# A transformer block with conditioned norms: all softmax sums inverted on VectorE, and a feed-forward step's weights in two transfers

## The chip, the cores and the metric

The kernel runs on one core of one Trainium2 chip. A core has five engines that run their own instruction streams and wait for each other through semaphores: TensorE (PE in the profile; its weight loads are PEld), VectorE (DVE), ScalarE (ACT), GpSimd (POOL) and SyncE (SP), which here only issues transfers. SP, ACT and POOL issue transfers to the same 16 DMA engines. The metric is the device time of one execution in microseconds, of which the median over several runs is compared.

## The reference

`x` has 4 sequences of 1024 tokens with 512 features, all in float32. One transformer block is computed and added to its input:

```python
def _tc_rmsnorm(x, t, gw, gb, bw, bb):
    g = (t @ gw.T + gb)[:, None, :]
    b = (t @ bw.T + bb)[:, None, :]
    inv_rms = rsqrt(mean(x * x, axis=-1, keepdims=True) + 1e-6)
    return g * x * inv_rms + b

x1 = x + attention(_tc_rmsnorm(x, t, g1w, g1b, b1w, b1b))    # 16 heads of 32, softmax over all 1024 keys
x2 = x1 + swiglu(_tc_rmsnorm(x1, t, g2w, g2b, b2w, b2b))     # (silu(x @ gate.T) * (x @ hid.T)) @ out.T, 2048 hidden
return x + x2
```

The softmax is `exp(s - max) / sum(exp(s - max))`. The kernel doesn't divide each weight: it sums the exponentials over the keys, takes the inverse, and multiplies the attention output by it.

## The kernel before, in words

Tokens are cut into 8 blocks of 512 (`n`; `NBLK`), features into 4 chunks of 128, and the hidden features into 16 slices of 128 (`f`; `NF`). Activations lie with features on the 128 partitions and tokens along the row.

**Key steps.** The main loop runs over steps `g`. A step takes 256 keys of four heads against 256 queries. Four steps (`UN`; `kind = g % 4`) cover the 1024 keys: together they are one set `j` of sums (64 sets), and a group of four steps in the profile. Eight groups are a query block of 32 steps (`BS`). In step `g` PE makes the scores of step `g` (`scores`, L301); ACT copies them to SBUF (`keep`, L308); VectorE follows the running maximum (`running_max`, L313 and L316). Once the four steps of a set are there, PE transposes the maxima (`max_T`), VectorE reduces them and splits them in three bfloat16 parts (`parts`), PE transposes these (`parts_T`), ACT copies them (mT, L340), PE spreads them to all partitions (`spread`, L348) and ACT copies that (`shift`, L349). Five steps after the scores VectorE adds the negative maximum (`shifted`, L354) and ACT takes the exponential (`exponential`, L357); a step later PE multiplies with the values (`weighted`, L367), and a transfer issued by POOL accumulates the exponentials of a set into its first tile (`accumulate`, L381). VectorE folds the two halves (`fold_sum`, L389).

**The inverse of the sums.** At `kind == 0` three groups after the scores, `sums` (L399) adds over the keys with a matmul against ones, so that each head's 256 sums stand on 32 equal rows. `sums_out` (L406) copies them from PSUM (L408). For 55 of the 64 sets they then go by transfers: `compact` (L148) stores one row per head to DRAM from ACT's queue; two steps later `take` (L153), on ACT's queue, loads the 1024 sums as 128 rows of 8; `invert` (L160) takes the reciprocal of these on VectorE; `put` (L164), on ACT's queue in the next group's `kind == 0`, stores them; `sums_in` (L414), at that group's `kind == 1`, loads each head's inverses back onto 32 rows with four broadcast transfers on SP's queue (L173); `normalize` (L424) multiplies at that group's `kind == 3`. The last set of each query block but the last (`near`, L402), seven in all, skips the transfers: VectorE takes the reciprocal of all rows at `kind == 1` (L821), and `normalize` follows at `kind == 2`. The last two sets (`direct`) are inverted straight from PSUM (`inverse`, L419) at once.

**The feed-forward part.** From step `FS` = 60 on, two steps make a pass `p` (128 passes: 16 slices for each of 8 token blocks). A pass computes the gate and hidden features of one slice by a scheme with seven products in place of eight: it takes sums of weight quarters and sums of token quarters. The weight sums are made once, in steps 4 to 51: `weight_sums` (L470) loads the slice's gate and hid weights at the end of step `3f + 4`, and at the end of step `3f + 6` VectorE forms four sums and SP stores them to DRAM (`s_w`). `load_f` (L502) fetches a pass's weights in two parts of two transfers each, part 1 of pass `p + 1` in its even step and part 0 of pass `p + 2` in its odd step. The pass runs `pair_26`, `copy_156` (L545), `pair_7`, `sub_5` (L552) in the even step, and `pair_3`, `gate_tanh` (L562), `pair_15` of the next pass, `take_5` (L526), `gate` (L567), `add_15` (L530), `pair_4`, `hidden` (L570) in the odd one. The even step also holds `contract` with the output weights of an earlier pass, which `take_contract` (L583) adds to the residual.

**What sets the order.** The order on PE, VectorE, ACT and POOL is that of the program. Beside the steps, fixed actions are hung on step numbers (`pin` at the start of a step, `between` halfway, `after` at its end), and a queue of matmul chains (projections of queries, keys and values, 1.5 a step) fills the steps before `FS`. Keys are asked for three steps ahead of use, values three, queries two, the residual (`load_res`, 1 MB) at the seventh step of a query block. SP issues loads and stores in its own order, each once its tile is free.

**Buffers.** Tiles of one tag share a ring. Tag `fw` (five of 4 KB a partition) holds `wkq`, the weights and sums in `weight_sums`, and the weights of the passes. Tag `h` (seven of 2 KB) holds what the projections stage for their stores before `FS`, and the hidden features after it. Tag `w` is two PSUM banks for sums, projections, `pa` and `pc`.

Of the kernel before, what the change touches and what calls it, by code (L numbers as in the profile page):

```python
# [10 lines left out]
F32 = mybir.dt.float32  # L11
BF16 = mybir.dt.bfloat16
AF = mybir.ActivationFunctionType
ALU = mybir.AluOpType
# [3 lines left out]
P = 128  # L18
# [6 lines left out]
def tile_cond_transformer_block(  # L25
# [122 lines left out]
    def compact(tag: str, t, rows: int, n: int):  # L148

        inv_s[tag] = tc.dram_tile([P // rows, n], F32, name=f"sums{tag}")  # L150
        nc.scalar.dma_start(out=inv_s[tag], in_=t[0:P:rows, :])
# [17 lines left out]
    def spread_inverse(tag: str, t, rows: int, n: int):  # L169

        src = inv_s.pop(tag).rearrange("(h p) c -> h (p c)", p=rows)
        for h in range(P // rows):
            nc.sync.dma_start(  # L173
                out=t[h * rows : (h + 1) * rows, :], in_=src[h : h + 1, :].to_broadcast([rows, n])
            )
# [47 lines left out]
    def load_wkq(hg: int):  # L223
        t = sb.tile([P, 2, C, P], F32, tag="fw", name=f"wkq{hg}", bufs=5)
        nc.sync.dma_start(out=t, in_=kq_w[hg])
        wkq[hg] = t
# [164 lines left out]
    def take_av(j: int):  # L391
        avs[j] = sb.tile([P, HQ], F32, tag="avs", name=f"avs{j}", bufs=3)
        nc.scalar.copy(avs[j], av.pop(j))
# [7 lines left out]

    def near(j: int):  # L402

        return j % (C * NB // HQ) == C * NB // HQ - 1 or j >= NR // UN - 2

    def sums_out(j: int):  # L406
        t = sb.tile([P, HQ], F32, tag="rec", name=f"total{j}", bufs=2)
        nc.scalar.copy(t, state.pop(("sum", j)))  # L408
        if near(j):
            state["rec", j] = t  # L410
        else:
            compact(f"s{j}", t, DH, HQ)

    def sums_in(j: int):  # L414
        t = sb.tile([P, HQ], F32, tag="rec", name=f"rec{j}", bufs=2)
        spread_inverse(f"s{j}", t, DH, HQ)
        state["rec", j] = t

    def inverse(j: int):  # L419
        rec = sb.tile([P, HQ], F32, tag="rec", name=f"rec{j}", bufs=2)  # L420
        nc.vector.reciprocal(rec, state.pop(("sum", j)))  # L421
        state["rec", j] = rec

    def normalize(j: int):  # L424

        m, qh = divmod(j, NB // HQ)
        n, hg = divmod(m, C)
        rec = state.pop(("rec", j))
        if (n, hg) not in oT:
            oT[n, hg] = sb.tile([P, NB], F32, tag=f"oT{hg}", name=f"oT{m}")  # L430
        nc.vector.tensor_tensor(oT[n, hg][:, qh * HQ : (qh + 1) * HQ], avs.pop(j), rec, ALU.mult)

# [37 lines left out]
    def weight_sums(f: int, step: int):  # L470
        if step == 0:
            state["gh", f] = sb.tile([P, 2, C, P], F32, tag="fw", name=f"gh{f}", bufs=5)
            nc.sync.dma_start(out=state["gh", f], in_=gh_w[f])
        else:
            t = state.pop(("gh", f))
            a11, a12, a21, a22 = (t[:, i, k : k + 2, :] for i in range(2) for k in (0, 2))
            o = sb.tile([P, 4, 2, P], F32, tag="fw", name=f"s{f}", bufs=5)
            nc.vector.tensor_tensor(o[:, 0], a21, a22, ALU.add)
            nc.vector.tensor_tensor(o[:, 1], o[:, 0], a11, ALU.subtract)
            nc.vector.tensor_tensor(o[:, 2], a11, a21, ALU.subtract)  # L480
            nc.vector.tensor_tensor(o[:, 3], a12, o[:, 1], ALU.subtract)
            nc.sync.dma_start(out=s_w[f], in_=o)

# [17 lines left out]

    def load_f(p: int, part: int):  # L502
        f = p % NF
        fw[p, part] = sb.tile([P, 4, 2, P], F32, tag="fw", name=f"fw{p}_{part}", bufs=5)
        if part == 0:
            nc.sync.dma_start(out=fw[p, 0][:, 0:2], in_=gh_w[f][:, 0].rearrange("p (a c) o -> p a c o", a=2))
            nc.sync.dma_start(out=fw[p, 0][:, 2:4], in_=s_w[f][:, 0:2])
        else:
            nc.sync.dma_start(out=fw[p, 1][:, 0:2], in_=s_w[f][:, 2:4])
            nc.sync.dma_start(out=fw[p, 1][:, 2], in_=gh_w[f][:, 1, 2:4])  # L510

# [6 lines left out]
    def pair_15(p: int):  # L518
        b11 = tokens(p // NF)[0]
        a = bank_a[p] = ps.tile([P, NB], F32, tag="w", name=f"pa{p}")  # L520
        product(a[:, LEFT], fw[p, 0][:, 0], b11, True)
        product(a[:, RIGHT], fw[p, 0][:, 2], state["sums"][:, 0])

# [8 lines left out]
    def pair_26(p: int):  # L532
        a = bank_a[p]
        product(a[:, LEFT], fw[p, 0][:, 1], tokens(p // NF)[2])
        product(a[:, RIGHT], fw[p, 0][:, 3], state["sums"][:, 1])

# [10 lines left out]
    def pair_7(p: int):  # L547
        product(bank_b[p][:, RIGHT], fw[p, 1][:, 0], tokens(p // NF)[1])

# [4 lines left out]
    def pair_3(p: int):  # L554
        product(bank_a[p][:, RIGHT], fw[p, 1][:, 1], tokens(p // NF)[3])

    def pair_4(p: int):
        product(bank_b[p][:, LEFT], fw[p, 1][:, 2], state["sums"][:, 2])

# [143 lines left out]
    with tc.manual_schedule(  # L703
# [59 lines left out]

        def take_sums(j: int, j_before: int):

            if 0 <= j < NR // UN:
                sums(j)
                if j >= direct:
                    inverse(j)
                    normalize(j)  # L770
                else:
                    sums_out(j)
            if 0 <= j_before < direct and not near(j_before):
                put(f"s{j_before}")

        while g < END:
# [8 lines left out]
            n_on = 0 <= j_n < NR // UN  # L785
            j_o = g // UN - 4
            o_on = 0 <= j_o < direct
            ffn = g >= FS
# [8 lines left out]
            if kind == 1 and m_on:  # L797
                spread(j_m, 0)
            if kind == 3 and o_on and not near(j_o):
                normalize(j_o)  # L800
            if kind == 2 and n_on and near(j_n) and j_n < direct:
                normalize(j_n)
            if x_on and kind != 1:
# [14 lines left out]
            if g < NR:  # L818
                keep(g)
            if kind == 1 and n_on and near(j_n) and j_n < direct:  # L820
                nc.vector.reciprocal(state["rec", j_n], state["rec", j_n])  # L821
            if kind == 2 and n_on and not near(j_n):
                take(f"s{j_n}")
            if kind == 1 and s_on:
                take_av(j_s)
            due = bool(first) and first[0][0] <= g
            if not ffn:
# [3 lines left out]
                if kind == 0:  # L831
                    take_sums(j_n, j_o)
                if g < NR:
# [17 lines left out]
                if kind == 3 and s_on:  # L851
                    fold_sum(j_s)
                if g in (FS - 4, FS - 3):
                    load_f(0, g - FS + 4)
                if g == FS - 1:
                    load_f(1, 0)
            elif even:
                load_f(p + 1, 1)
                pair_26(p)
                copy_156(p)  # L860
                if kind == 0:
                    take_sums(j_n, j_o)
                if x_on:
# [16 lines left out]
            else:  # L880
                load_f(p + 2, 0)
                extra = due or len(queue) > FG
# [36 lines left out]
                for fn, a in halfway.pop(g, []):  # L919
                    fn(*a)  # L920
            if kind == 3 and n_on and not near(j_n):
                invert(f"s{j_n}")
            if kind == 1 and o_on and not near(j_o):
                sums_in(j_o)
            columns[0] = DH
# [13 lines left out]
        for p in range(p0, NP_):  # L939
            if p + 1 < NP_:  # L940
                load_f(p + 1, 1)
            pair_26(p)
            copy_156(p)
            if p == n * NF - 1:
                token_sums(n, 0)
                token_sums(n, 1)
                token_sums(n, 2)
            one, two, evict = filler(p, True)
            one()
            if p + 2 < NP_:  # L950
                load_f(p + 2, 0)
            pair_7(p)
            sub_5(p)
            pair_3(p)
            gate_tanh(p)
            gate(p)
            if p + 1 < NP_:
                pair_15(p + 1)
                take_5(p + 1)
                add_15(p + 1)  # L960
            pair_4(p)
            hidden(p)
            if p == n * NF - 1:
                token_sums(n, 3)
            two()
            evict()
            if p == p0:
                pm = ps.tile([P, NB], F32, tag="w", name=f"pmf{n}")
                for c in range(C):
                    nc.tensor.matmul(pm, ones_mean, squares[c], start=(c == 0), stop=(c == C - 1))  # L970
                inv = sb.tile([P, NB], F32, tag="tot", name=f"invf{n}", bufs=1)
                nc.scalar.activation(inv, pm, AF.Sqrt, bias=eps)
                nc.vector.reciprocal(inv, inv)
                state[f"f{n}"] = inv
            if p == p0 + 1:
                norm_rest(1, n // QB, x2[n], f"f{n}")
# [45 lines left out]
```

## Time and profile before

| | |
|---|---|
| median of 3 runs | 2523.32 us (2521.0 to 2535.55) |
| the profiled execution | 2529.8 us, its span 2528.0 us, mean granted clock of TensorE 0.986 |
| busy before 553 us (474 us from 79 on): PE, DVE, ACT | 447.1, 370.0, 330.2 us; DMA share 0.91 |
| busy from 553 to 2212 us (1659 us) | 1585.1, 1351.5, 996.9 us; DMA share 0.85 |
| busy from 2212 us to the end (316 us) | 303.3, 109.7, 49.9 us; DMA share 0.42 |
| transfers of sums | 165 from ACT's queue (4 KB each), 220 from SP's (32 KB each) |
| transfers of a pass's weights | 512: 256 of `fw<-sw`, 128 and 128 of `fw<-in_gh_w` |
| reciprocals | 55 of 128x8 (192 ns), 7 of 128x256 from SBUF (1744 ns), 2 from PSUM (1752 ns) |

A row such as `L354 DVE TENSOR_TENSOR raw<-raw,shift 128x2048 f32 ... x320 | 593.0, 1854 | 158.4 <-ACT shift L349 153.2` names the line, the engine, the operation, what it writes and reads by the program's tile names, how often, then busy us and mean ns of one, and the idle time of the engine just ahead of it with what ended most of it. In the timeline a bracket gives the idle time and its releaser. A q behind an engine's name (ACTq, SPq) marks what its sequencer does, such as issuing a transfer. PEclk is the share of TensorE's clock that was granted. The DMA share is the mean busy share of the 16 DMA engines.

### The profile page before, as it was taken

Reading aid. Unit: us, or ns where it says so; the run is one execution under the profiler, and the core shown is the slowest. Engines: PE = TensorE matmul, PEld = TensorE weight load, DVE = VectorE, ACT = ScalarE, POOL = GpSimd, SP = SyncE. Lnnn points to the kernel's source line nnn. Section 1 sums busy time; section 2 is a strip of 40 time slices with the busy share of each in tenths; the row PEclk is TensorE's granted clock in tenths of the full one; section 3 lists DMA queues with packets and bytes.
Section 4 is the critical chain, followed back from the end, with each engine's and each line's share of the span. In section 5 each row is a group of like instructions: output and inputs, shape, how many; then the busy total and the mean of one; then the engine's idle time right before and its main releaser. Section 6 shows DMA issues by size and latency. Waiting matters only on the chain. (4 is left out here: it accounts for less than half of the span.)

```text
span 2528.0 us, 72020 instructions
## 1 busy us (share of the span) xinstructions
PE 2404.4 (95%) x31749; PEld 1131.5 (45%) x31749; DVE 1854.4 (73%) x2180; ACT 1409.2 (56%) x1486; POOL 172.8 (7%) x207
## 2 busy tenths in 40 slices
PE   8989999999999899998999899989999899989999
PEld 3333333344444444544444444444444444434444
DVE  2677878777879786997788778978798768843332
ACT  3667776676556565665566556655565556512110
POOL 0000000000000000000000000000000000000000
PEclk9999999999999999999999999999999999999999
DMA  6599998999878887898879888888788888863442
GB/s 208 158 283 248 254 248 235 231 225 224 216 191 209 222 200 187 214 219 200 196 198 220 209 191 196 220 215 200 192 216 206 202 196 196 212 165 114 143 124 84
DMA packets 245085, 509.68 MB, mean 202 GB/s; under 512 B 44483, under 2 KB 125471, under 8 KB 217382
## 3 DMA queue, kind: packets, MB, share of 16 engines
q0 software_dynamic: 28656, 208.68, 42.8%
q1 hardware_dynamic: 197520, 295.66, 35.8%
q8 instruction: 251, 4.11, 0.6%
q10 hardware_dynamic: 18598, 0.74, 0.5%
q14 instruction: 60, 0.49, 0.1%
HBM read 253.87 MB, written 42.42 MB: 117 GB/s over the span
## 5 line engine op out<-in xcount | busy, mean ns | idle before, releaser
L354 DVE TENSOR_TENSOR raw<-raw,shift 128x2048 f32<-128x2048 f32 (+1 forms) x320 | 593.0, 1854 | 158.4 <-ACT shift L349 153.2
L357 ACT ACTIVATE raw<-raw 128x2048 f32<-128x2048 f32 x256 | 490.9, 1917 | 245.2 <-DVE raw L354 127.2
L308 ACT COPY raw<-sc 128x2048 f32<-128x2048 f32 x256 | 479.5, 1873 | 184.0 <-PE sc L301 147.4
L313 DVE TENSOR_TENSOR rmax<-rmax,raw 128x1024 f32<-128x1024 f32 x384 | 469.0, 1221 | 68.3 <-ACT raw L308 62.6
L106 PE MATMUL pc<-h,ow 128*32 128x512 f32 x4096 | 471.0, 597 | 7.5 <-DVE rec L421 5.0
L106 PE MATMUL pa<-x,fw 128*32 128x256 f32 x6144 | 388.4, 386 | 5.2 <-DVE pa L530 5.1
L367 PE MATMUL av<-raw,v 128*32 128x256 f32 x4096 | 278.4, 390 | 29.0 <-ACT raw L357 22.6
L381 POOL DMA_DIRECT2D raw<-raw x192 | 165.6, 863 | 2040.0 <-ACT raw L357 931.6
L301 PE MATMUL sc<-q,k 32*128 32x256 f32 x4096 | 293.3, 400 | 1.0 <-ACT raw L308 1.0
L106 PE MATMUL pa<-sums,fw 128*32 128x256 f32 x4096 | 268.0, 379 | 0.0
L106 PEld LDWEIGHTS pa<-x,fw 128*32 128x32 f32 x6144 | 193.1, 111 | 166.4 <-issue 30.5
L106 PEld LDWEIGHTS pc<-h,ow 128*32 128x32 f32 x4096 | 128.2, 110 | 254.1 <-issue 225.4
L106 PE MATMUL pkq<-y,wkq 128*32 128x512 f32 (+1 forms) x1664 | 231.6, 594 | 6.6 <-ACT y L187 4.1
L301 PEld LDWEIGHTS sc<-q,k 32*128 32x128 f32 x4096 | 184.9, 184 | 116.9 <-issue 68.7
L367 PEld LDWEIGHTS av<-raw,v 128*32 128x32 f32 x4096 | 107.9, 110 | 154.7 <-ACT raw L357 47.0
L106 PEld LDWEIGHTS pa<-sums,fw 128*32 128x32 f32 x4096 | 133.3, 110 | 88.9 <-issue 1.4
L545 ACT COPY pb<-pa 128x256 f32<-128x256 f32 x128 | 46.3, 362 | 203.2 <-PE pa L106 163.4
L583 DVE SCALAR_TENSOR_TENSOR res<-pc,res 128x512 f32<-128x512 f32 x128 | 88.1, 688 | 86.8 <-PE pc L106 86.7
L562 ACT ACTIVATE t<-pa 128x512 f32<-128x512 f32 x128 | 77.9, 608 | 109.5 <-PE pa L106 109.5
L106 PE MATMUL pb<-x,fw 128*32 128x256 f32 x2048 | 134.1, 379 | 4.2 <-ACT pb L545 4.1
L106 PE MATMUL pb<-sums,fw 128*32 128x256 f32 x2048 | 133.9, 379 | 0.0
L106 PEld LDWEIGHTS pkq<-y,wkq 128*32 128x32 f32 (+1 forms) x1664 | 73.3, 116 | 133.9 <-issue 121.8
(105 smaller groups left out, 1933.5 us busy)
## 6 DMA issues: line engine op xcount, KB each, us to landing
raw<-raw POOLq DMA_DIRECT2D x192, 1024.0 KB, 8.9
fw<-sw SPq DMA_DIRECT2D x256, 256.0 KB
fw<-in_gh_w SPq DMA_DIRECT2D x128, 256.0 KB
ow<-in_out_w SPq DMA_DIRECT2D x128, 256.0 KB
wkq<-in_kq_w SPq DMA_DIRECT2D x32, 512.0 KB
v<-vs SPq DMA_DIRECT2D x128, 128.0 KB
fw<-in_gh_w SPq DMA_DIRECT2D x128, 128.0 KB
k<-kqs SPq DMA_DIRECT2D x124, 128.0 KB
```

What stands on the lines that cost most here:

```text
L106: nc.tensor.matmul(dst[k : k + n, :], w[:, k : k + n], moving, start=start, stop=stop, skip_group_check=seeded)
L301: nc.tensor.matmul(sc[:, i, k, :], keys[rows, k * P : (k + 1) * P], queries[rows, :], start=True, stop=True)
L308: nc.scalar.copy(raw[r].rearrange("p k h q -> p h k q"), state.pop(("sc", r)))
L313: nc.vector.tensor_tensor(rmax[j], rmax[j], raw[r][:, k, :, :], ALU.max)
L354: nc.vector.tensor_tensor(t, t, s.unsqueeze(1).to_broadcast(list(t.shape)), ALU.add)
L357: nc.scalar.activation(raw[r], raw[r], AF.Exp)
L367: nc.tensor.matmul(av[j][i * DH : (i + 1) * DH, :], v[m, u][:, k, i * DH : (i + 1) * DH], raw[r][:, k, i, :], start=(kt == 0), stop=(kt == ...
L381: nc.gpsimd.dma_start(out=acc[j].rearrange("p k h q -> p (k h q)"), in_=raw[r].rearrange("p k h q -> p (k h q)"), accum_op=ALU.add,)
L545: nc.scalar.copy(bank_b[p][:, RIGHT], bank_a[p][:, RIGHT])
L562: nc.scalar.activation(state["t", p], bank_a[p], AF.Tanh, scale=0.5)
L583: nc.vector.scalar_tensor_tensor(r, pp, 0.5, r, ALU.mult, ALU.add)
```

## The change

Every set of sums is now copied from PSUM to SBUF by ACT and inverted in place by VectorE on all 128 rows (128x256); `near`, `sums_in` and the transfers for sums are gone. The reciprocal stands at the start of `kind == 2` ahead of `shifted`, `normalize` right behind it, but for the first set of a query block, whose `normalize` comes at `kind == 1` of the next group. The last two sets are inverted at once, as before, but from the copy. The weights of a pass come in two transfers: three quarters of the gate and hid weights (`fa`, 3 KB a partition), which the host has put in a row, and all four sums (`fw`, 4 KB). Both are asked for at the start of the even step of pass `p`, for pass `p + 2`. The tiles of `weight_sums` are halved and move from tag `fw` to tag `h`. Rings: `fw` from five to three (for `wkq` and the sums), `fa` new with three, `avs` from three to two. The transfers for the norms' roots are as before.

```diff
-        t = sb.tile([P, 2, C, P], F32, tag="fw", name=f"wkq{hg}", bufs=5)
+        t = sb.tile([P, 2, C, P], F32, tag="fw", name=f"wkq{hg}", bufs=3)
...
-        avs[j] = sb.tile([P, HQ], F32, tag="avs", name=f"avs{j}", bufs=3)
+        avs[j] = sb.tile([P, HQ], F32, tag="avs", name=f"avs{j}", bufs=2)
...
     def sums_out(j: int):
-        t = sb.tile([P, HQ], F32, tag="rec", name=f"total{j}", bufs=2)
-        nc.scalar.copy(t, state.pop(("sum", j)))
-        if near(j):
-            state["rec", j] = t
-        else:
-            compact(f"s{j}", t, DH, HQ)
-
-    def sums_in(j: int):
-        t = sb.tile([P, HQ], F32, tag="rec", name=f"rec{j}", bufs=2)
-        spread_inverse(f"s{j}", t, DH, HQ)
-        state["rec", j] = t
+        state["total", j] = sb.tile([P, HQ], F32, tag="total", name=f"total{j}", bufs=2)
+        nc.scalar.copy(state["total", j], state.pop(("sum", j)))
 
     def inverse(j: int):
-        rec = sb.tile([P, HQ], F32, tag="rec", name=f"rec{j}", bufs=2)
-        nc.vector.reciprocal(rec, state.pop(("sum", j)))
-        state["rec", j] = rec
+        nc.vector.reciprocal(state["total", j], state["total", j])
...
         if step == 0:
-            state["gh", f] = sb.tile([P, 2, C, P], F32, tag="fw", name=f"gh{f}", bufs=5)
-            nc.sync.dma_start(out=state["gh", f], in_=gh_w[f])
+            for i in range(2):
+                state["gh", f, i] = sb.tile([P, 2, 2, P], F32, tag="h", name=f"gh{f}_{i}", bufs=7)
+                nc.sync.dma_start(out=state["gh", f, i], in_=gh_w[f][:, 2 * i : 2 * i + 2])
...
+            o = [sb.tile([P, 2, 2, P], F32, tag="h", name=f"s{f}_{i}", bufs=7) for i in range(2)]
...
-            nc.sync.dma_start(out=s_w[f], in_=o)
+            for i in range(2):
+                nc.sync.dma_start(out=s_w[f][:, 2 * i : 2 * i + 2], in_=o[i])
...
-    def load_f(p: int, part: int):
+    def load_f(p: int):
         f = p % NF
-        fw[p, part] = sb.tile([P, 4, 2, P], F32, tag="fw", name=f"fw{p}_{part}", bufs=5)
-        if part == 0:
-            nc.sync.dma_start(out=fw[p, 0][:, 0:2], in_=gh_w[f][:, 0].rearrange("p (a c) o -> p a c o", a=2))
-            nc.sync.dma_start(out=fw[p, 0][:, 2:4], in_=s_w[f][:, 0:2])
-        else:
-            nc.sync.dma_start(out=fw[p, 1][:, 0:2], in_=s_w[f][:, 2:4])
-            nc.sync.dma_start(out=fw[p, 1][:, 2], in_=gh_w[f][:, 1, 2:4])
+        fw[p, 0] = sb.tile([P, 3, 2, P], F32, tag="fa", name=f"fa{p}", bufs=3)
+        nc.sync.dma_start(out=fw[p, 0], in_=gh_w[f][:, 0:3])
+        fw[p, 1] = sb.tile([P, 4, 2, P], F32, tag="fw", name=f"fw{p}", bufs=3)
+        nc.sync.dma_start(out=fw[p, 1], in_=s_w[f])
...
                 sums(j)
+                sums_out(j)
                 if j >= direct:
                     inverse(j)
                     normalize(j)
-                else:
-                    sums_out(j)
-            if 0 <= j_before < direct and not near(j_before):
-                put(f"s{j_before}")
...
-            if kind == 3 and o_on and not near(j_o):
-                normalize(j_o)
-            if kind == 2 and n_on and near(j_n) and j_n < direct:
-                normalize(j_n)
+
+            if kind == 2 and n_on and j_n < direct:
+                inverse(j_n)
+                if j_n % (BS // UN):
+                    normalize(j_n)
+            if kind == 1 and n_on and j_n % (BS // UN) == 1:
+                normalize(j_n - 1)
...
-            if kind == 1 and n_on and near(j_n) and j_n < direct:
-                nc.vector.reciprocal(state["rec", j_n], state["rec", j_n])
-            if kind == 2 and n_on and not near(j_n):
-                take(f"s{j_n}")
...
-                if g in (FS - 4, FS - 3):
-                    load_f(0, g - FS + 4)
-                if g == FS - 1:
-                    load_f(1, 0)
+                if g in (FS - 4, FS - 2):
+                    load_f((g - FS + 4) // 2)
             elif even:
-                load_f(p + 1, 1)
+                load_f(p + 2)
...
             else:
-                load_f(p + 2, 0)
...
-            if kind == 3 and n_on and not near(j_n):
-                invert(f"s{j_n}")
-            if kind == 1 and o_on and not near(j_o):
-                sums_in(j_o)
...
+    gh = np.stack([inputs_first(given["gate_w"]), inputs_first(given["hid_w"])], axis=2)
...
-        "gh_w": np.stack([inputs_first(given["gate_w"]), inputs_first(given["hid_w"])], axis=2),
+        "gh_w": gh.reshape(*gh.shape[:2], 4, 2, P)[:, :, [0, 1, 3, 2]],
```

More of the change, by code (lines that the diff above doesn't have):

```diff
@@ L400, in sums @@
         state["sum", j] = total
-    def near(j: int):
-        return j % (C * NB // HQ) == C * NB // HQ - 1 or j >= NR // UN - 2
     def sums_out(j: int):
-        t = sb.tile([P, HQ], F32, tag="rec", name=f"total{j}", bufs=2)
-        nc.scalar.copy(t, state.pop(("sum", j)))
-        if near(j):
-            state["rec", j] = t
-        else:
-            compact(f"s{j}", t, DH, HQ)
-    def sums_in(j: int):
-        t = sb.tile([P, HQ], F32, tag="rec", name=f"rec{j}", bufs=2)
-        spread_inverse(f"s{j}", t, DH, HQ)
-        state["rec", j] = t
+        state["total", j] = sb.tile([P, HQ], F32, tag="total", name=f"total{j}", bufs=2)
+        nc.scalar.copy(state["total", j], state.pop(("sum", j)))
     def inverse(j: int):
-        rec = sb.tile([P, HQ], F32, tag="rec", name=f"rec{j}", bufs=2)
-        nc.vector.reciprocal(rec, state.pop(("sum", j)))
-        state["rec", j] = rec
+        nc.vector.reciprocal(state["total", j], state["total", j])
     def normalize(j: int):
@@ L427, in normalize @@
         n, hg = divmod(m, C)
-        rec = state.pop(("rec", j))
+        total = state.pop(("total", j))
         if (n, hg) not in oT:
             oT[n, hg] = sb.tile([P, NB], F32, tag=f"oT{hg}", name=f"oT{m}")
-        nc.vector.tensor_tensor(oT[n, hg][:, qh * HQ : (qh + 1) * HQ], avs.pop(j), rec, ALU.mult)
+        nc.vector.tensor_tensor(oT[n, hg][:, qh * HQ : (qh + 1) * HQ], avs.pop(j), total, ALU.mult)
     def load_res(n: int):
@@ L471, in weight_sums @@
         if step == 0:
-            state["gh", f] = sb.tile([P, 2, C, P], F32, tag="fw", name=f"gh{f}", bufs=5)
-            nc.sync.dma_start(out=state["gh", f], in_=gh_w[f])
-        else:
[L475 to L481, printed above, removed]
-            nc.sync.dma_start(out=s_w[f], in_=o)
+            for i in range(2):
+                state["gh", f, i] = sb.tile([P, 2, 2, P], F32, tag="h", name=f"gh{f}_{i}", bufs=7)
+                nc.sync.dma_start(out=state["gh", f, i], in_=gh_w[f][:, 2 * i : 2 * i + 2])
+        else:
+            (a11, a12), (a22, a21) = (
+                (t[:, 0], t[:, 1]) for t in (state.pop(("gh", f, i)) for i in range(2))
+            )
+            o = [sb.tile([P, 2, 2, P], F32, tag="h", name=f"s{f}_{i}", bufs=7) for i in range(2)]
+            nc.vector.tensor_tensor(o[0][:, 0], a21, a22, ALU.add)
+            nc.vector.tensor_tensor(o[0][:, 1], o[0][:, 0], a11, ALU.subtract)
+            nc.vector.tensor_tensor(o[1][:, 0], a11, a21, ALU.subtract)
+            nc.vector.tensor_tensor(o[1][:, 1], a12, o[0][:, 1], ALU.subtract)
+            for i in range(2):
+                nc.sync.dma_start(out=s_w[f][:, 2 * i : 2 * i + 2], in_=o[i])
     def tokens(n: int):
@@ L521, in pair_15 @@
         product(a[:, LEFT], fw[p, 0][:, 0], b11, True)
-        product(a[:, RIGHT], fw[p, 0][:, 2], state["sums"][:, 0])
+        product(a[:, RIGHT], fw[p, 1][:, 0], state["sums"][:, 0])
     def take_5(p: int):
@@ L534, in pair_26 @@
         product(a[:, LEFT], fw[p, 0][:, 1], tokens(p // NF)[2])
-        product(a[:, RIGHT], fw[p, 0][:, 3], state["sums"][:, 1])
+        product(a[:, RIGHT], fw[p, 1][:, 1], state["sums"][:, 1])
     def copy_156(p: int):
@@ L547, in pair_7 @@
     def pair_7(p: int):
-        product(bank_b[p][:, RIGHT], fw[p, 1][:, 0], tokens(p // NF)[1])
+        product(bank_b[p][:, RIGHT], fw[p, 1][:, 2], tokens(p // NF)[1])
     def sub_5(p: int):
@@ L554, in pair_3 @@
     def pair_3(p: int):
-        product(bank_a[p][:, RIGHT], fw[p, 1][:, 1], tokens(p // NF)[3])
+        product(bank_a[p][:, RIGHT], fw[p, 1][:, 3], tokens(p // NF)[3])
     def pair_4(p: int):
-        product(bank_b[p][:, LEFT], fw[p, 1][:, 2], state["sums"][:, 2])
+        product(bank_b[p][:, LEFT], fw[p, 0][:, 2], state["sums"][:, 2])
     def gate_tanh(p: int):
@@ L762, in filler, with take_sums @@
             )
-        def take_sums(j: int, j_before: int):
+        def take_sums(j: int):
             if 0 <= j < NR // UN:
                 sums(j)
+                sums_out(j)
                 if j >= direct:
@@ L785, in tile_cond_transformer_block @@
             n_on = 0 <= j_n < NR // UN
-            j_o = g // UN - 4
-            o_on = 0 <= j_o < direct
             ffn = g >= FS
@@ L831, in tile_cond_transformer_block @@
                 if kind == 0:
-                    take_sums(j_n, j_o)
+                    take_sums(j_n)
                 if g < NR:
@@ L861, in tile_cond_transformer_block @@
                 if kind == 0:
-                    take_sums(j_n, j_o)
+                    take_sums(j_n)
                 if x_on:
@@ L939, in tile_cond_transformer_block @@
         for p in range(p0, NP_):
-            if p + 1 < NP_:
-                load_f(p + 1, 1)
+            if p + 2 < NP_:
+                load_f(p + 2)
             pair_26(p)
@@ L949, in tile_cond_transformer_block @@
             one()
-            if p + 2 < NP_:
-                load_f(p + 2, 0)
             pair_7(p)
```

## The prediction

> **What bounds the kernel now.** I read the page first (engines' busy shares), then the waits of TensorE (PE), then the timeline at its longest gaps, then the busy time in stretches of four key steps.
>
> ```profile
> PE 2404.4 (95%) x31749; PEld 1131.5 (45%) x31749; DVE 1854.4 (73%) x2180; ACT 1409.2 (56%) x1486; POOL 172.8 (7%) x207
> ```
>
> PE is busy for 95%, so at most 2528.0 - 2404.4 = 123.6 us of its gaps can be won, plus what it loses while its clock is low. PE's waits (who waited for whom: us in total, times, longest) say what the gaps are, and the longest wait of ScalarE (ACT) on a transfer, in the same view of all engines, what lies behind them.
>
> ```profile
> PE sp L348 <- ACT mT L340: 49.1, 8, 11.3
> PE av L367 <- ACT raw L357: 22.6, 23, 1.5
> ...
> PE pa L106 <- DVE pa L530: 5.1, 13, 0.7
> PE pc L106 <- DVE rec L421: 5.0, 2, 3.2
> ...
> PE pb L106 <- ACT pb L545: 4.1, 4, 1.6
> ```
>
> ```profile
> ACT raw L357 <- DMA sumss<-total: 79.7, 19, 15.4
> ```
>
> The 49.1 us are in essence five gaps of 9.78, 8.70, 8.26, 8.83 and 11.28 us, one in each of five query blocks. The timeline of the first (start, us, engine, line, operation):
>
> ```profile
> 871.04 0.37 ACT L408 COPY total<-sum 128x256 f32<-128x256 f32 x1
> ...
> 872.61 0.38 SPq L290 DMA_DIRECT2D v<-vs  x1
> 873.05 0.42 SPq L285 DMA_DIRECT2D q<-kqs  x1
> ...
> 879.17 0.50 ACTq L151 DMA_DIRECT2D sumss<-total  x1
> 884.64 0.32 ACTq L167 DMA_DIRECT2D invss<-fews  x1
> 885.29 1.91 ACT L357 ACTIVATE raw<-raw 128x2048 f32<-128x2048 f32 x1 [13.88 <-DMA sumss<-total]
> 887.11 0.35 ACT L340 COPY mT<-pt 12x256 bf16<-12x256 bf16 x1
> ...
> 887.51 0.58 PE L348 MATMUL sp<-mT,select 12*128 12x256 bf16 x2 [9.78 <-ACT mT L340]
> ```
>
> ACT has the sums at 871.41, yet its store of them is issued at 879.17 and that of the inverses at 884.64. The trace's semaphores say why: SyncE's and ACT's transfers take turns on eight completion semaphores; the store's is still held by the load of values issued at 872.61 (landed 879.10), the other's by the load of queries (landed 884.56). [...]Behind ACT's waiting issue stand the exponential and the copy of mT, and PE waits for that. Stretches (length, busy us of each engine, PEclk, DMA share) of a plain group of four key steps, of the group with the gap, and of the one after it:
>
> ```profile
> 836.90:866.70 29.80, 29.80 (x446) 15.27 (x442) 26.10 (x31) 19.28 (x20) 2.58 (x3) 1.00 0.89 221
> 866.70:909.10 42.40, 32.62 (x442) 15.81 (x438) 26.20 (x31) 19.10 (x20) 2.58 (x3) 0.84 0.78 191
> 909.10:939.70 30.60, 29.99 (x446) 15.17 (x442) 27.47 (x33) 19.27 (x20) 2.59 (x3) 1.00 0.84 201
> 1045.60:1075.30 29.70, 29.70 (x442) 15.23 (x438) 27.10 (x34) 19.88 (x22) 2.59 (x3) 1.00 0.91 218
> ```
>
> Without a gap a group is 29.7 us of pure PE. With it 42.4, and PEclk says that half of the clock was gone for some 13.6 us too. Note the DVE column: VectorE has 26 to 27 us of work in 29.7.
>
> **The change part by part: what it removes.** (1) For 55 of the 64 sums, three ACT transfers and four SyncE transfers each; no sums transfer is left on ACT to wait. By the starts of the scores, the five groups with a gap take 42.44, 41.61, 41.00, 41.74 and 42.98 us, together 209.8; five plain ones are 5 x 29.73 = 148.7. Gain 61.1. (2) In each block's sixth group ACT's copy pb (L545) is late behind the same issues: its third step takes 0.45, 0.27, 1.31, 0.20, 0 and 1.77 over the plain 8.10. Gain 4.0. (3) The group at 604.7 takes 34.00, 4.3 over a plain one. PE waits there 2.5 us for the first `ow` load, and ACT sits 6.9 for its store. That load comes late on SyncE either way: I take 2, between 0 and 4.3. (4) The last two sums were inverted straight from PSUM, and PE waited 5.0 us for the bank; now ACT copies them out (0.37). The first of these waits also cost 3.4 us at half clock. Gain 5.5, between 3 and 6.7. (5) Before 553 us, ACT's waits for its own issues (5.2 at 219, several of 2 to 4 between 469 and 520) stand beside PE gaps of 3.6, 3.7 and 1.2: I take 5, between 0 and 8. Sum 77.6.
>
> **What it adds.** Row by row (group, busy us and mean ns):
>
> ```profile
> L162 DVE RECIPROCAL fews<-fews 128x8 f32<-128x8 f32 x55 | 10.5, 192 | 0.0
> ...
> L821 DVE RECIPROCAL total<-total 128x256 f32<-128x256 f32 x7 | 12.2, 1744 | 0.0
> ```
>
> 55 x (1744 - 192) = 85.4 us more on VectorE. It is put ahead of `shifted` of the third step, with `normalize` (0.41) moved up beside it from the fourth: 2.16 us. Behind it on VectorE stand `shifted`, the running maxima, `take_contract` and `sub_5`; for `shifted` waits ACT's exponential, for that PE's `weighted`. In the plain group: `shifted` ends 858.47, the exponential runs 858.51 to 860.42, `weighted` starts 862.22. Slack 1.8, so 2.16 makes PE wait 0.33. Then `add_15` (L530), at 867.13, comes 1.75 later and ends 869.30, while `pair_26`, 868.64 + 0.33, must wait for it until 869.35: 0.38 more. Together 0.7. The third stretch above is a check: its group already holds one such reciprocal (at a different step) and takes 30.55 instead of 29.73: 0.8, with 0.61 of PE waiting for L530. I take 0.75.
>
> For the eight groups of a block, slack as above: groups 0, 1, 5, 7 have 1.8 (5 without its ACT delay): 0.75 each. Group 2 has its reciprocal already: 0. Group 3 holds the output projection, slack 4.2: 0. Groups 4 and 6 have other VectorE work there, slack 0.65: 1.45 at `weighted` and 0.25 at `add_15`, 1.7 each. A block: 6.4. Six blocks: 38. Lower end: VectorE's delay is caught up but in groups 4 and 6, 6 x 3.4 = 20. Upper: every group is bound by VectorE, 7 x 1.55 x 6 = 65.
> Before 553 us the same slack is 2.4 to 6.7 but in three groups (1.2, 0.6, 1.8): 1.0 + 1.6 + 0.3 = 2.9. I take 5; at most 12 x 1.55 = 19.
>
> [...]after the 2.5 us gap at 610.0, 3.4 us at half clock, but none after gaps of 1.8. [...]my waits of up to 1.5 us cost no clock. Should they add to 2.6 in groups 4 and 6, [...]the trace 12 x 1.7 = 20 us more; I go by the trace, and leave that to the upper end.
>
> **What it moves.** Weights: two transfers of 384 and 512 KB a pass for four of 128 to 256 KB, 896 KB either way. [...]The trace has no wait of PE for fw at all, so I count 0. What hides them is lead: loads were issued one pass (about 15 us) ahead of use, and are now issued one and a half ahead, at the start of pass p for p + 2, once `pair_4(p-1)` has freed `fa`. SyncE stands there, with keys, values, `ow` behind it; these are asked for up to three steps (24 us) ahead, and the slowest load above took 11.5. If that cover fails PE waits a few us per block; upper end 6 x 4.
>
> Weight sums leave the `fw` ring for the seven `h` buffers, with the projections' staging. Per three steps the ring takes 4 such tiles and about 4.5 staged ones: seven turn over in 2.5 steps or 20 us, where they had 40. A buffer whose store hasn't landed holds up ACT or SyncE. Landings above took 6.5 to 11.5 us, so mostly covered: 3, between 0 (or -3: `wkq` no longer waits for weight sums, 26.8 us on SyncE) and 5 a round, 16 x 5 = 80. The `wkq` ring of three keeps its two-ahead loading: 0, with that same upper end. `avs` of two: the one late `normalize` of a block stands before the next `take_av`: 0 to 0.4.
>
> **Sum.** 77.6 - 38 - 5 - 3 = 31.6. The profiled execution took 2529.8 (span 2528.0): 2498.2. The median of the runs is 2523.3, 0.9974 of it: 2492.
>
> **Rivals.**
> Cheap VectorE (0.15): slack is found that I don't see, only groups 4 and 6 pay, and the staging ring nothing. 77.6 - 20 - 3 = 55: 2469. For it: TensorE's wait for L530 is 5.1 us in all, seven reciprocals included. Against: the 0.8 in the third stretch.
> Full VectorE, or the transfers themselves (0.17): VectorE at 28.6 of 29.7 us has nothing to catch up in, 65 + 19 + 3 against 77.6: 2532. Or the stall wasn't ACT's issue but the burst of loads, and PE next waits for keys or weights there: 40 of the 61 come back, 2532 as well. Against it: PE shows no wait for either.
> Slower (0.09): the staging ring starves. Stage one (553 us) has a DMA share of 0.91; if each of the 16 rounds waits for a store, at 5 us, 80 comes on: 2492 + 77 = 2569. It decides once landings exceed about 16 us (20 less the half step to the store's issue). To be slower by over 1% it must cost 57 us, 3.6 a round.
>
> **Numbers.** My forecast has 0.59: 2492, itself from 2475 to 2510. 1% (25 us) is about what a measurement of this kernel can tell from no change. Faster: cheap VectorE and four fifths of mine, 0.62. Same: the rest of mine and the third case, 0.29. Slower 0.09. The range 2458 to 2535 leaves out the slower case, a third of the one before it and a little of the cheap one: not quite 2 in 10.
>
> **What would show it.** Right: no ACT wait on `sumss`, no PE gap over 4 us in the steady part, those five groups near 30.5 us, clock 1.0 there; PE's waits for raw L357 and pa L530 up by some 25 and 10 us; VectorE busy near 1940. Wrong: PE waits for fw, keys or values; steps before 553 us longer, with st or sv waiting for stores; groups 0 and 7 over 31.3.

## The result and the profile after

The changed kernel takes 2496.57 us (median of 4 runs, 2495.65 to 2498.47), the kernel before 2522.16 in the same comparison (4 runs, 2518.41 to 2535.55): a ratio of 0.989, with a 95% interval of 0.9853 to 0.9927. The forecast of 2492 is 4.6 us off. The gain is 1.1%, small, but clear of no change by the interval. The profiled execution of after took 2495.65 us, its span is 2493.8, its mean granted clock 0.998 (0.986 before).

The page's line of busy times, after:

```profile
PE 2392.5 (96%) x31749; PEld 1125.5 (45%) x31749; DVE 1941.8 (78%) x2180; ACT 1406.4 (56%) x1488; POOL 172.4 (7%) x207
```

VectorE has 87.4 us more, nearly all from 55 long reciprocals in place of short ones (85.2); PE is busy 11.9 us less with as many matmuls; from 60 us on its clock was halved for 61.4 us in before and, but for the last 2 us, not at all in after. The new row among the groups of operations (line, engine, operation, count, then busy us, mean ns and idle time just ahead):

```profile
L407 DVE RECIPROCAL total<-total 128x256 f32<-128x256 f32 x64 | 111.4, 1741 | 0.8 <-ACT total L404 0.8
```

The view of waits, after (who waits for whom: us in total, times, longest):

```profile
ACT raw L357 <- DVE raw L354: 321.0, 173, 6.4
```

the same row before:

```profile
ACT raw L357 <- DVE raw L354: 127.2, 97, 4.8
```

and TensorE's own part of that view, after:

```profile
PE av L367 <- ACT raw L357: 55.1, 67, 2.4
PE pa L106 <- DVE pa L515: 8.0, 42, 0.2
PE pma L106 <- ACT total L404: 7.6, 5, 1.7
...
PE pc L106 <- ACT total L404: 1.1, 2, 0.6
PE pc L106 <- DMA ow<-in_out_w: 1.1, 1, 1.1
```

The five long waits for mT are gone, and so is every wait for a transfer of sums. In their place ACT waits 321.0 us for VectorE's `shifted` where it waited 127.2, and PE 55.1 us for ACT's exponential where it waited 22.6: 67 waits of 0.3 to 1.5 us (one of 2.4), instead of five of 8.3 to 11.3. The busy time in stretches of four key steps: a plain group, the one that had the gap, and the groups with index 4 and 6 of a block (length, busy us of PE, PEld, DVE, ACT, POOL, PEclk, DMA share, GB/s):

```profile
838.70:869.20 30.50, 30.01 (x442) 15.13 (x438) 27.62 (x31) 19.18 (x20) 2.58 (x3) 1.00 0.89 213
869.20:899.70 30.50, 30.01 (x442) 15.13 (x438) 27.62 (x31) 19.18 (x20) 2.58 (x3) 1.00 0.96 255
974.40:1008.00 33.60, 31.06 (x454) 15.34 (x450) 26.56 (x30) 22.18 (x23) 2.58 (x3) 1.00 0.73 173
1038.50:1070.20 31.70, 30.00 (x446) 15.13 (x442) 29.96 (x36) 20.87 (x23) 2.58 (x3) 1.00 0.81 196
```

and the group with index 4 before (that with index 6, 29.70 us, stands in the prediction):

```profile
983.50:1015.40 31.90, 30.83 (x450) 15.28 (x446) 24.78 (x30) 22.55 (x23) 2.58 (x3) 1.00 0.81 197
```

The group that took 42.4 us at a clock of 0.84 takes 30.50 at 1.00 and can't be told from its neighbour, at a DMA share of 0.96. The others pay for the reciprocal. How, the timeline of after shows (start, us, engine, line, operation, idle time and its releaser):

```profile
851.09 2.50 DVE L354 TENSOR_TENSOR raw<-raw,shift 128x1024 f32<-128x1024 f32 x2 [1.64 <-ACT shift L349]
...
858.37 1.74 DVE L407 RECIPROCAL total<-total 128x256 f32<-128x256 f32 x1
...
860.14 0.42 DVE L416 TENSOR_TENSOR oT<-avs,total 128x256 f32<-128x256 f32 x1
860.49 2.29 DVE L354 TENSOR_TENSOR raw<-raw,shift 128x2048 f32<-128x2048 f32 x1
...
862.81 1.91 ACT L357 ACTIVATE raw<-raw 128x2048 f32<-128x2048 f32 x1 [3.29 <-DVE raw L354]
...
864.77 1.07 PE L367 MATMUL av<-raw,v 128*32 128x256 f32 x16 [0.31 <-ACT raw L357]
...
871.56 1.07 PE L106 MATMUL pa<-x,fa 128*32 128x256 f32 x16 [0.19 <-DVE pa L515]
```

ACT stands idle for 3.29 us behind `shifted`, and PE for 0.31 and then 0.19. Note the first line: a step earlier VectorE had itself stood idle for 1.64 us, almost the length of the reciprocal.

Where the time went, from the starts of the scores' groups in each trace, in us:

| kernel | start | groups 0 to 15 | groups 16 to 62 | rest | span |
|---|---|---|---|---|---|
| before | 51.0 | 524.0 | 1581.4 | 371.6 | 2528.0 |
| after | 50.0 | 524.5 | 1550.9 | 368.4 | 2493.8 |
| `before_again` | 49.8 | 527.7 | 1581.4 | 370.6 | 2529.5 |
| `sums_only` | 50.1 | 528.7 | 1550.9 | 369.5 | 2499.2 |
| `weights_only` | 50.2 | 525.7 | 1538.2 | 370.2 | 2484.3 |
| `sp_queue` | 51.0 | 521.9 | 1518.9 | 372.0 | 2463.8 |
| `weights_sp` | 50.1 | 529.8 | 1519.8 | 374.8 | 2474.5 |
| `narrow` | 51.2 | 514.0 | 1511.2 | 365.8 | 2442.2 |
| `inverse_early` | 49.6 | 514.2 | 1518.3 | 371.0 | 2453.1 |

Groups 16 to 62 are the feed-forward part with attention beside it. The kernel before, profiled a second time, gave 1581.4 there again, but 3.7 more in the first sixteen groups: differences of that size in that column, from single profiles, prove nothing.

### The profile page after: what moved, and what is told of

Read it like the earlier page. It is cut to its first block, busy times and chain, and to the rows that moved or that the text cites. A ratio compares the mean times of both kernels' runs of the same rounds, so it can differ in the third digit from the quotient of the medians.

```text
span 2493.8 us, 71084 instructions
## 1 busy us (share of the span) xinstructions
PE 2392.5 (96%) x31749; PEld 1125.5 (45%) x31749; DVE 1941.8 (78%) x2180; ACT 1406.4 (56%) x1488; POOL 172.4 (7%) x207
## 5 line engine op out<-in xcount | busy, mean ns | idle before, releaser
L357 ACT ACTIVATE raw<-raw 128x2048 f32<-128x2048 f32 x256 | 490.9, 1918 | 321.2 <-DVE raw L354 321.0
L367 PE MATMUL av<-raw,v 128*32 128x256 f32 x4096 | 274.1, 385 | 61.5 <-ACT raw L357 55.1
L106 PE MATMUL pa<-x,fa 128*32 128x256 f32 x4096 | 269.1, 380 | 8.1 <-DVE pa L515 8.0
L106 PEld LDWEIGHTS pa<-x,fa 128*32 128x32 f32 x4096 | 127.5, 109 | 122.8 <-DVE pa L515 28.8
L106 PE MATMUL pa<-x,fw 128*32 128x256 f32 x2048 | 135.2, 381 | 0.0
L106 PE MATMUL pb<-sums,fa 128*32 128x256 f32 x2048 | 134.0, 379 | 0.0
```

The costliest lines, as they stand in the source:

```text
L106: nc.tensor.matmul(dst[k : k + n, :], w[:, k : k + n], moving, start=start, stop=stop, skip_group_check=seeded)
L357: nc.scalar.activation(raw[r], raw[r], AF.Exp)
L367: nc.tensor.matmul(av[j][i * DH : (i + 1) * DH, :], v[m, u][:, k, i * DH : (i + 1) * DH], raw[r][:, k, i, :], start=(kt == 0), stop=(kt == ...
```

## The experiments

**One part of the change alone.** `sums_only` has the new inverse, with the weights' transfers, rings and sums as before (two of the places in which it differs from the changed kernel):

```diff
-    def load_f(p: int):
+    def load_f(p: int, part: int):
...
-        t = sb.tile([P, 2, C, P], F32, tag="fw", name=f"wkq{hg}", bufs=3)
+        t = sb.tile([P, 2, C, P], F32, tag="fw", name=f"wkq{hg}", bufs=5)
```

> The sums' part of the change alone; weights and rings as before. If ACT's own issues behind slow loads were the loss (my theory), this has all of the gain: 2493 to 2501 us, no PE gap over 4 us after 60 us, plain groups of four key steps 30.5 us. If the fewer weight transfers carried part of the gain (rival), 2503 to 2515.

Measured: 2501.33 us, a ratio to the kernel before of 0.9899 (0.9885 to 0.9914). That is 0.3 us above the range that I expected. Its groups 16 to 62 are those of after to the tenth. What separates the two is mainly 4.2 us in the first sixteen groups, where this kernel has a 2.4 us wait of PE for `wkq` and 3.4 us at half clock more than after; that is about what two profiles of one kernel differ by there. So beside the new inverse two transfers for four are worth nothing in the steady part, as forecast, and at most some 5 us ahead of it.

`weights_only` has the new weights' transfers, rings and sums, and the inverse by transfers as before. To fit in SBUF, the tile `p5` has one buffer instead of two (two of the places in which it differs from the kernel before):

```diff
-        fifth[p] = sb.tile([P, HQ], F32, tag="p5", name=f"p5_{p}", bufs=2)
+        fifth[p] = sb.tile([P, HQ], F32, tag="p5", name=f"p5_{p}", bufs=1)
...
-    def load_f(p: int, part: int):
+    def load_f(p: int):
```

> The weights' part alone (two transfers a pass, weight sums in the staging ring; p5 one buffer instead of two, to fit); sums by transfers as before. My theory: ACT still waits at the residual load, with gaps of 5 us or more in at least three blocks, somewhat shorter since the transfer eight places back is older: 2505 to 2525 us. Rival (the weights carry the gain): under 2503, and the gaps gone.

Measured: 2485.21 us, 0.9837 (0.9817 to 0.9856). It is faster than the whole change, and my expectation missed by 20 us. Its five groups with a gap take 33.33, 34.22, 34.48, 33.31 and 33.59, together 168.9 against 209.8: these 40.9 us are as much as its whole gain (40.3). The timeline at the first of them, of `weights_only`:

```profile
869.10 0.33 SPq L435 DMA_DIRECT2D res<-in_x  x1
...
869.80 0.38 ACT L408 COPY total<-sum 128x256 f32<-128x256 f32 x1
...
870.20 0.51 ACTq L151 DMA_DIRECT2D sumss<-total  x1
...
875.80 0.32 ACTq L167 DMA_DIRECT2D invss<-fews  x1
...
876.16 1.91 ACT L357 ACTIVATE raw<-raw 128x2048 f32<-128x2048 f32 x1 [5.99 <-DVE pb L552]
...
878.38 0.37 PE L348 MATMUL sp<-mT,select 12*128 12x256 bf16 x2 [1.89 <-ACT mT L340]
```

The burst of loads behind the residual is still there. But SyncE issues fewer transfers, so ACT's two stand at other places in the turn of eight completion semaphores: the store finds one that came free at 869.09, when the store of `out` that held it landed, and goes straight after the copy, at 870.20; only the other waits, for the residual, issued eight places earlier, at 869.10, which landed at 875.72, 0.08 us ahead of the issue at 875.80 (the bracket names VectorE's `sub_5`, which happened to end 0.04 us later). The view of waits of `weights_only` has four more such waits of ACT for the residual, of 26.3 us together, the longest 7.0. ACT stands for 6.0 us instead of 13.9. The two parts of the change therefore mend the same stall and don't add up: 24 us alone and 40 us alone, 26 together. With the stall mostly cured by the weights' part, what the sums' part still adds is mainly VectorE's price.

**The cause of the stall.** `sp_queue` leaves everything as before, but SyncE issues the three transfers of a set's sums instead of ACT (the first of three such lines):

```diff
-        nc.scalar.dma_start(out=inv_s[tag], in_=t[0:P:rows, :])
+        (nc.sync if tag[0] == "s" else nc.scalar).dma_start(out=inv_s[tag], in_=t[0:P:rows, :])
```

> The kernel before with the three transfers of each set's sums issued by SP instead of ACT, nothing else. My theory (the loss is ACT standing in its own order behind an issue that waits): no PE gap over 4 us after 60 us and no VectorE price, 2450 to 2485 us. Rival (the burst of transfers stops PE whoever issues, or SP now stands behind the sums and keys, values or weights come late): new PE waits, 2500 or more.

Measured: 2464.62 us, 0.9751 (0.9725 to 0.9778). The timeline of `sp_queue` at the same place, and the stretch around it:

```profile
867.48 0.33 SPq L435 DMA_DIRECT2D res<-in_x  x1
...
869.00 1.91 ACT L357 ACTIVATE raw<-raw 128x2048 f32<-128x2048 f32 x1 [0.17 <-DVE raw L354]
...
870.23 0.45 SPq L167 DMA_DIRECT2D invss<-fews  x1
...
882.91 0.50 SPq L151 DMA_DIRECT2D sumss<-total  x1
```

```profile
864.10:893.80 29.70, 29.70 (x442) 15.22 (x438) 24.79 (x29) 18.31 (x19) 2.58 (x3) 1.00 0.86 204
```

The store of the sums is issued even later than before, at 882.91, and in this group nobody minds: ACT goes on with the exponential, and the group is pure PE. All five groups that had a gap are at 29.73. A little comes back behind them: the next group takes 30.88, 31.64 and 32.11 in the first three blocks, where it took 30.55, some 3 us in all. So what cost 61 us was neither the load on the DMA engines nor the lateness of the sums, but that a waiting issue stood in ACT's stream ahead of work that PE needed.

`res_late` was to take the residual's load out of the burst:

```diff
-        pin(g0 + 6, load_res, n)
+        pin(g0 + (10 if n < NBLK - 1 else 6), load_res, n)
```

> The kernel before with one number changed: the residual load is asked for four steps later, into a stretch where ACT issues no transfer of sums. My theory (ACT's issue waits for a load slowed by the residual's 1 MB): the five gaps go without any VectorE cost, 2455 to 2475 us. Rival (the burst on the DMA engines itself stops PE, whoever issues): the gaps move with the load, 2510 to 2530.

Measured: 2529.09 us, 1.0007 (0.9995 to 1.002). The timeline of `res_late`:

```profile
865.91 0.34 SPq L585 DMA_DIRECT2D out<-res  x1
...
875.37 0.33 SPq L435 DMA_DIRECT2D res<-in_x  x1
...
882.47 0.50 ACTq L151 DMA_DIRECT2D sumss<-total  x1
...
887.99 0.32 ACTq L167 DMA_DIRECT2D invss<-fews  x1
```

The load didn't move: it follows the store that frees its buffer, landed at 875.36, with the same transfers behind it as before. The time lies in my rival's range, but not for the rival's reason. So this run says nothing of the burst, only that the residual's time is set by its buffer and not by the step it is pinned to. Before, the seven loads issued behind the residual from 872.61 to 876.45 took 6.5 to 11.6 us to land. Which share of that is due to the residual's 1 MB, and which to SyncE's standing still for 10 us and then issuing eight loads in 5, stays open.

`weights_sp` joins the weights' part with the sums on SyncE's queue (the edits of `weights_only` and `sp_queue`).

> The weights' part alone, with the sums' three transfers issued by SP. If the remaining waits of the weights-only kernel (2485) are ACT's issues too: 2440 to 2470 us, close to the kernel with narrow reciprocals (2443). If SP's own order now costs: 2485 or more.

Measured: 2478.11 us, 0.9818 (0.9785 to 0.985), 13 us slower than `sp_queue` alone, and between my two forecasts. Its feed-forward part is as good (1519.8), but the first sixteen groups take 7.9 more. The timeline of `weights_sp` at its longest wait there:

```profile
206.89 0.58 ACT L263 COPY sv<-pv 128x512 f32<-128x512 f32 x1 [10.00 <-DMA kqs<-st]
...
209.30 2.09 PE L301 MATMUL sc<-q,k 32*128 32x256 f32 x16 [5.16 <-ACT raw L308]
```

ACT's copy of staged values waits 10 us for the store of an earlier staged tile to land, and PE 5.16 us behind it. That is the starving ring of the prediction's slower rival, in a kernel that loads SyncE's queue more; in `weights_only` the longest such wait is 4.5 us. In the view of waits of after there is no wait of ACT for any such store.

**VectorE's price.** `narrow` is the changed kernel, but the reciprocal takes 8 of the 256 columns; the other 248 are left without their inverse, so part of the computation is left out:

```diff
-        nc.vector.reciprocal(state["total", j], state["total", j])
+        nc.vector.reciprocal(state["total", j][:, :8], state["total", j][:, :8])
```

> The changed kernel with the reciprocal on 8 of 256 columns, the other 248 left out: VectorE's price by itself. My theory (0.75 us in a plain group, 1.7 in two of eight, 6.7 a block measured): 40 us in the six blocks and 0 to 5 before them, so 2450 to 2460 us and plain groups of 29.7. If most of VectorE's delay is caught up elsewhere: 2475 or more.

Measured: 2443.46 us, 0.967 (0.9655 to 0.9684). A plain group of `narrow`:

```profile
853.80:883.50 29.70, 29.70 (x442) 15.22 (x438) 26.15 (x31) 19.19 (x20) 2.59 (x3) 1.00 0.93 247
```

The long reciprocal costs 2496.57 - 2443.46 = 53 us. By the table 39.7 of it lie in groups 16 to 62, 10.5 ahead of them and 2.6 at the end. I had expected 2450 at least, with up to 5 us ahead of them.

`inverse_early` pays this price where nothing waits: the reciprocal goes one step earlier, into the idle time of 1.64 us seen above, while `normalize` stays.

```diff
-            if kind == 2 and n_on and j_n < direct:
+            if kind == 1 and n_on and j_n < direct:
                 inverse(j_n)
-                if j_n % (BS // UN):
-                    normalize(j_n)
+            if kind == 2 and n_on and j_n < direct and j_n % (BS // UN):
+                normalize(j_n)
```

> The changed kernel with the reciprocal one step earlier: at the second step of the group, ahead of `shifted`, where VectorE idles 1.64 us for ACT's copy of the shift; `normalize` stays where it is. If what counts is the place (VectorE's idle time is there to be used): plain groups from 30.5 back to 29.8, 2468 to 2485 us in all. If VectorE is simply full, so that 1.74 us cost the same anywhere: 2492 to 2500.

Measured: 2452.53 us (2449.38 to 2454.94), 0.9702 (0.968 to 0.9724), the fastest kernel here that computes all of the reference, and 15 us below the range that I expected. The timeline and a plain group of `inverse_early`:

```profile
866.51 1.74 DVE L407 RECIPROCAL total<-total 128x256 f32<-128x256 f32 x1
...
868.24 2.50 DVE L354 TENSOR_TENSOR raw<-raw,shift 128x1024 f32<-128x1024 f32 x2
...
875.52 0.41 DVE L416 TENSOR_TENSOR oT<-avs,total 128x256 f32<-128x256 f32 x1
875.85 2.29 DVE L354 TENSOR_TENSOR raw<-raw,shift 128x2048 f32<-128x2048 f32 x1
```

```profile
856.30:886.00 29.70, 29.70 (x442) 15.21 (x438) 27.58 (x31) 19.22 (x20) 2.58 (x3) 1.00 0.90 232
```

VectorE works as much as in after (27.6 us), and PE doesn't wait. So VectorE's load as such cost next to nothing; its place in the order cost 44 of the 53 us (by the medians of two comparisons; by the ratios, 0.989 - 0.9702 = 0.019 of the 0.022 that `narrow` saves). What it still takes over `narrow` is, by the table, 7.1 us in groups 16 to 62 and 5.2 at the end, where PE once waits 3.4 us for VectorE's `fold_sum`; the mean granted clock is 0.995, where it is 0.998 in after.

`before_again` is the kernel before, unchanged, profiled once more to see where its runs differ, by up to 17 us.

> The kernel before, unchanged, for a second profile. My theory of its spread (2519 to 2535 us): the five gaps differ from execution to execution, the rest doesn't. So its five groups with a gap sum to another value than 209.8 us, by about as much as its span differs from 2528.0, and a plain group is 29.73 again. If the spread came from elsewhere, the five sum to 208 to 212 with another span.

Measured: 2531.28 us. Its five groups with a gap take 41.21, 42.15, 43.53, 42.03 and 40.77, together 209.7, as in the first profile (209.8), though each is different. The two spans differ by 1.5 us only, so this says little of a spread of 17: it isn't shown to come from there, and where it comes from stays open.

## Why the prediction was right

**The stall (1), 61.1: right in size and in cause, but not in what removes it.** The five groups fell from 209.8 to 152.5, which is 61.1 less 5 x 0.77 for the reciprocal. That ACT's waiting issue was the loss, not the burst, is shown by `sp_queue`. What I didn't see is that the other part of the change would move the turns of the semaphores and cure two thirds of it as well: I counted the weights' transfers at 0 in the steady part, which holds only because the sums' part had already taken the stall away. The likeliest case was right for both together, and would have been some 40 us out for the weights alone.

**The small gains.** Of (2), pb, and (3), the group at 604.7, 4.0 and 2 were forecast: PE's waits for pb shrank from 4.1 to 1.2, and that group went from 34.00 to 31.28, 2.7. (4), the inverse at the end, was put at 5.5: `narrow`, where VectorE's price is out, has a last part 5.8 shorter than before. After keeps 3.2 of it, since two inverses are still on the path there; I had counted that at 0.

**VectorE's price: right in the feed-forward part, too low before it.** Forecast 38, measured 39.7. By group of a block, 0 to 7, forecast 0.75, 0.75, 0, 0, 1.7, 0.75, 1.7, 0.75; measured 0.77, 0.77, -0.05, 0.40, 1.55, 0.77 over a plain group, 1.97 and 0.52: 6.7 for 6.4. The way was right too: in a plain group PE falls 0.37 us behind `narrow` at `weighted` and 0.40 more at the next pair, where 0.33 and 0.38 were forecast. Of the signs, PE's waits for the exponential rose by 32.5 (25 forecast), but those for `add_15` (L515 now) by 2.9 only (10 forecast): in a plain group PE is also busy for 30.01 us where it was for 29.70, so part of the delay doesn't count as a wait. For the first sixteen groups I took 5 between 0 and 19; it was about 10.5. That is the term most out. The slack that I read there, 2.4 to 6.7 us, was that of a kernel which stood waiting for transfers; with those waits gone, part of the slack went too. This last reason is argued and wasn't tested by itself, and fits in part at best: 7.0 of the 10.5 lie in the groups with index 5, 8 and 11, and of these before took 2.4 and 0.7 longer than `narrow` in two, but 0.25 less in that with index 8.

**Staging ring 3, early gain 5.** Together with VectorE's 5 they made +3 for the first sixteen groups; +0.5 was measured. That this came near is luck, as the errors cancel: without VectorE's price (`narrow`) that part is 10.0 shorter than before, where I had -2 for the gain and the ring together. How these 10 divide between the two isn't settled, within the 3.7 that profiles differ by.

**The rivals.** Cheap VectorE at 2469 fell by its place in the order, not by its work: with the reciprocal one step earlier the kernel goes below 2469. Full VectorE or the transfers at 2532 fell by the stretches: no new wait for keys or weights, at a DMA share of 0.96. The slower case was not met in after. A single such wait shows in `weights_sp`, where it costs PE 5.16 us.

**The sum.** The forecast against the profiled execution was 2529.8 - 31.6 = 2498.2; measured 2495.65, and the spans differ by 34.2. By parts, 29.1 us were forecast and 30.5 measured in groups 16 to 62, 3 lost and 0.5 lost ahead of them, 5.5 and 3.2 gained behind them; the first scores start 1.0 earlier, which wasn't forecast. The step to 2492 then scaled by the median of the runs before, which took off 6 us. Without it the forecast would have been 1.6 us too high instead of 4.6 too low: after's runs lie within 2.8 us of each other, the profiled one lowest.

## What to carry to other kernels

When a stall has a transfer's issue at its root, ask first which engine's stream the issue stands in: moving three lines to another queue gave 63 us, the rebuilt algorithm 26. Before putting new work on a nearly full engine, look for the wait that this engine itself has in each step, and place the work there: the same reciprocal cost 53 us behind that wait and 9 us in it. And two parts that mend the same stall don't add; run each alone before both are kept.

## What the runs showed of the hardware

**Clock after short gaps.** I had taken the drop to half clock to follow gaps of 2.5 us (at 610.0 in the trace of before, 3.4 us at half clock) and not of 1.8 (1.87 at 2245.8), though the same trace has one of 2.43 at 130.5 without a drop. One gap that occurs in two kernels at the same point of the work, PE's wait for the exponential of 2.44 us at 309.3 in after and 2.46 at 311.8 in `sums_only`, tells another story. The stretches of 10 us around it, of after and of `sums_only`:

```profile
308.00:318.00 10.00, 7.56 (x86) 3.63 (x83) 7.65 (x6) 8.12 (x9) 0.86 (x1) 1.00 0.93 263
```

```profile
310.50:320.50 10.00, 7.54 (x74) 2.79 (x72) 7.46 (x5) 7.53 (x7) 0.86 (x1) 0.83 0.98 247
```

PEclk is 1.00 in one and 0.83 in the other (3.4 us at half clock). In `inverse_early` a wait of 1.88 us comes once a block; the first and the second of them:

```profile
717.50:727.50 10.00, 8.12 (x96) 3.79 (x92) 6.45 (x8) 7.97 (x9) 0.00 (x0) 0.83 0.19 69
976.60:986.60 10.00, 8.12 (x116) 3.64 (x112) 6.45 (x8) 7.89 (x9) 0.00 (x0) 1.00 0.18 58
```

PEclk is 0.83 around the first and 1.00 around the second. In these traces waits of 1.9 and of 2.4 to 2.5 us thus came with a drop and without one: the length alone didn't decide, and what else did was not shown. That my waits of up to 1.5 us would cost no clock was an estimate from the trace of before; in after, with 67 waits for the exponential, the clock stayed at 1.00 from 20.5 to 2491.8 us.

**Two queues, one turn of semaphores.** In the trace of before SyncE's 1433 transfers and ACT's 188 take turns on the same eight completion semaphores, and ACT was held by loads that SyncE had issued eight places earlier: its store was issued at 879.17, 0.07 us after the load of values landed, and the store of the inverses at 884.64, 0.08 us after that of queries. ACT stood for 13.88 us there, and for 5.99 in `weights_only`, where SyncE issues fewer transfers and the two places were those of the store of `out` and the residual's load. In `sp_queue` the exponential has no wait for a transfer.
